# A graph layer's edge sort: scan operands moved to PSUM in three pieces, sums in a bank of their own, nodes to be normed in three buffers

## The chip, the cores and the metric

The kernel runs on one core of one Trainium2 chip. A time is the device time of one execution in microseconds. TensorE is PE in the profile (PEld is its loading of weights), VectorE is DVE, ScalarE is ACT, GpSimd is POOL and SyncE is SP. Each engine works through its own queue in order and waits on semaphores; SP only issues DMAs here, ACT and POOL issue some too.

## The reference

One layer of a graph network over N = 12,500 nodes of 64 features and E = 212,500 edges:

```python
h = jnp.maximum(_layernorm(x, axis=-1), 0.0)
edge_in = jnp.concatenate([h[row], h[col], dist], axis=1)      # row = src, col = dst
e = jax.nn.silu(edge_in @ eW1 + eb1)
e = jax.nn.silu(e @ eW2 + eb2)
agg = jax.ops.segment_sum(e, row, num_segments=h.shape[0])
out = jax.nn.silu(jnp.concatenate([h, agg], axis=1) @ nW1 + nb1) @ nW2 + nb2
return x + out
```

The edges come sorted by `dst`, while the sums go by `src`; `dist` is `edge_weight1`. The hidden width is 128.

## The kernel before, in words

**Node tables.** The nodes stand in NB = 100 buckets of L = 125 (node n is in bucket n mod 100). For twelve buckets at a time `normed` loads rows of x into one of two buffers `xs`, and norms them (`norm`: mean L531, difference L534, squares on ScalarE L535, variance, L543). `products` then turns four buckets (transposes L550, copy L554) and multiplies them with the two halves of eW1 (L180). The half for `src` is written out as three BF16 parts (`ta`, L598), that for `dst` as F32 (`tb`, L591). These generators, nine groups of twelve buckets, form the `feed`; `groups` lists them and `turns` takes a step of up to three of them in turn. The load of the next group stands in the same generator as its norm: it is issued, and the norm's first instruction is recorded one step later.

**Sending edges to their bucket.** The edges are cut into 208 blocks of 1024, and the blocks into 11 chunks (8 blocks, then 20 each). For a block, `count` compares (L308 makes `pick`, L309 makes `oh`, one row for each of the 100 buckets with a one where an edge belongs to that bucket), runs a scan along the block (L319, `run`: how many edges of this chunk the bucket has had so far, in two halves of 512), and multiplies the scan with `oh` (L323, `own`: the rank of each edge in its bucket's row). `send` sums `own` over the buckets with eight small matmuls (L342, into eight columns of `misc`), adds the bucket's base (L362, `to`: the row in DRAM to write), makes each edge's first-layer part from its `dst` node's row and its weight (L350, L357, L366), and scatters 128 edges an instruction to `q` in DRAM with GpSimd's indirect DMA (L371, 1,661 in all). `to` has four buffers, `qs` eight.

**The sums.** When all scatters of a chunk have landed, its 25 batches of four buckets are fetched (L416 the edges, L421 the `src` table) and go through a pipeline of steps of four tiles: `s_lr` and `s_one_t` (L439, L444) build the one-hot of `src`, `s_pt` (L453, L460) adds the parts of the first layer, ScalarE applies SiLU (L464), `s_p2` is the second layer (L492, L496), `s_one` (L473) a one-hot of the other orientation, `s_seg` (L504) sums the messages by node into PSUM, and `s_add` (L515) adds a batch's sums to `aggT` in SBUF. With the last chunk the node network runs too (`nodes`). Chunk c is summed while chunk c + 1 and later ones are counted and sent.

**Order.** PE, DVE, ACT and SP run in the order in which the program records them. The main loop walks over a list `turn` of pipeline steps with four hooks (`None`); at a hook it records pieces of `count` and `send` as far as a line between `marks` says, and two steps of the `feed`. A piece pairs one step of `count(s + 1)` with one of `send(s)`: in the first L308 and L309 with the rank matmuls, in the second the first half's scan and product with L350, L362 and four scatters, in the third the other half with four scatters. Ahead of the loop, chunk 0 and nine pieces of chunk 1 are recorded with four steps of the `feed` each.

**PSUM.** All eight banks are in use: `mm` four, `p2` two, and two of the pool `sgp`. In one of these stands the tile `misc`, which holds the sums of `s_seg` (500 columns, named `seg`) and the ranks (8 columns); in the other `run` (512 columns). Waits are made for tiles, so that one part of `misc` waits for the other. `nil`, a column of zeros and the scan's second input, is in SBUF.

Of the kernel before, what the change touches and what calls it, by code (L numbers as in the profile page):

```python
# [28 lines left out]
F32 = mybir.dt.float32  # L29
# [4 lines left out]
OP = mybir.AluOpType  # L34
# [4 lines left out]
P = 128  # L39
L = 125  # L40
WL = 48
HB = 64
BLK = 1024
HALF = BLK // 2
TB = BLK // P
PAIR = 2 * BLK
G = 4
# [12 lines left out]
def tile_gnn(ctx: ExitStack, tc: tile.TileContext, x, src, dst, ew, eW1, eb1, eW2, eb2, nW1, nb1, nW2, nb2, out):  # L60
    nc = tc.nc
    N, D = x.shape
    H = eW2.shape[0]
    E = src.shape[0]
    assert D == 64 and H == P and N % L == 0
    NB = N // L
# [40 lines left out]
    CH = 12  # L107
# [19 lines left out]
    for a in range(2):  # L127
        half = slice(a * D, (a + 1) * D)
# [62 lines left out]
    for win in wins:  # L191
        nc.vector.memset(win, 0.0)
        for a in range(2):
            for i, row in enumerate((w1d, eb1b)):
                at = a * HB + WL + i
# [40 lines left out]
    cnt = ctx.enter_context(tc.tile_pool(name="cnt", bufs=1))  # L236
    qsp = ctx.enter_context(tc.tile_pool(name="qs", bufs=8))
    top = ctx.enter_context(tc.tile_pool(name="to", bufs=4))
    with ExitStack() as work:
        mm = work.enter_context(tc.tile_pool(name="mm", bufs=4, space=PSUM))  # L240
        p2p = work.enter_context(tc.tile_pool(name="p2", bufs=2, space=PSUM))
        sgp = work.enter_context(tc.tile_pool(name="sg", bufs=1, space=PSUM))
# [2 lines left out]
                engines={mybir.EngineType.PE, mybir.EngineType.DVE, mybir.EngineType.Activation, mybir.EngineType.SP}  # L245
            )
        )
        misc = sgp.tile([P, G * L + TB], F32, name="misc")
        seg = misc[:, : G * L].rearrange("p (b l) -> p b l", l=L)
        rank = misc[:, G * L :]  # L250
        run = sgp.tile([NB, HALF], F32, name="run")
        oh = cnt.tile([NB, BLK], F16, name="oh")
        nil = cnt.tile([NB, 1], F32, name="nil")
        nc.vector.memset(nil, 0.0)
        carry = {}
        blk = {}
        nblocks = -(-E // BLK)
# [44 lines left out]
        def count(s):  # L302

            if s >= nblocks:
                return
            c = chunk_of[s]
            bc, bb, win, pick = blk[s]
            nc.vector.tensor_scalar(pick, bc, same, plus, op0=OP.is_equal, op1=OP.add)  # L308
            nc.vector.tensor_scalar(oh, bb[:NB, :], part[:NB, :], None, op0=OP.is_equal)  # L309
            yield  # L310
            weights(s)
            own = wk.tile([NB, BLK], F16, name="own")
            blk[s].append(own)
            for h in range(2):
                half = slice(h * HALF, (h + 1) * HALF)
                n = min(HALF, E - s * BLK - h * HALF)
                if n <= 0:
                    break
                nc.vector.tensor_tensor_scan(  # L319
                    run, oh[:, half], nil.to_broadcast([NB, HALF]), carry.get(c, -1.0), op0=OP.add, op1=OP.add  # L320
                )
                end = carry[c] = run[:, n - 1 : n]
                nc.vector.tensor_tensor(own[:, half], run, oh[:, half], op=OP.mult)  # L323
                if h == 0:
                    yield
            if s + 1 == nblocks or chunk_of[s + 1] != c:
                u = wk.tile([NB, 1], F32, name="u")
                for limit, op in ((chunks[c][2] * P - 1, OP.is_gt), (chunks[c][3] - 1, OP.is_lt)):
                    nc.vector.tensor_scalar(u, end, float(limit), None, op0=op)
                    nc.vector.tensor_tensor(bad[:NB, 1:2], bad[:NB, 1:2], u, op=OP.add)  # L330
            yield
# [70 lines left out]
        batch, st = {}, {}  # L402
# [3 lines left out]
        def fetch(i):  # L406
            if i >= len(batches):
                return
            c, B, n = batches[i]
            assert pending[c] == 0  # L410
            while B not in done_a:
                next(feed)
            q = chunks[c][-1]
            at = B * G * n * P
            qt = ld2.tile([P, G * most, W], F32, name="qt")
            nc.sync.dma_start(  # L416
                qt[:, : G * n, :].rearrange("p j w -> p (j w)"),
                q[at : at + G * n * P, :].rearrange("(p j) w -> p (j w)", p=P),
            )
            a3 = ld2.tile([P, G, 3, H], BF16, name="a3")  # L420
            nc.sync.dma_start(  # L421
                a3.rearrange("l b s f -> l b (s f)"), ta_buckets[:, B * G : B * G + G]
            )
            batch[c, B] = [qt, a3]
            if c == len(chunks) - 1:
                node_in[B] = nodes_in(B, ndp[0])

        def of(k):

            c, B, n, g = steps[k]  # L430
            return batch[c, B], [((g * G + t) % n * G + (g * G + t) // n, (g * G + t) // n) for t in range(G)]

        def s_lr(k):
            (qt, _), tiles = of(k)
            loc = qt.rearrange("p j w -> p (j w)").bitcast(BF16)
            lr = mm.tile([P, G, P], F32, name="lr", tag="mm")
            for t, (j, _) in enumerate(tiles):
                at = 2 * (j * W + H) + 1
                nc.tensor.matmul(lr[:L, t, :], loc[:, at : at + 1].to_broadcast([P, L]), identb, start=True, stop=True)  # L439
            st[k] = {"lr": lr}  # L440
# [5 lines left out]

        def s_pt(k):

            (qt, a3), tiles = of(k)
            oneT = st[k].pop("oneT")  # L450
            pt = mm.tile([P, G, P], F32, name="pt", tag="mm")
            for t, (j, _) in enumerate(tiles):
                nc.tensor.matmul(  # L453
                    pt[:, t, :], qt[:, j, :H], ident, is_transpose=True, start=t == 0, stop=False, skip_group_check=True
                )
            for b, same in itertools.groupby(range(G), lambda t: tiles[t][1]):
                same = list(same)
                cols = slice(same[0], same[-1] + 1)
                for i in range(3):
                    nc.tensor.matmul(  # L460
                        pt[:, cols, :], a3[:L, b, i, :], oneT[:, cols, :], start=False, stop=i == 2, skip_group_check=True
                    )
            e1 = wk.tile([P, G, P], F32, name="e1")
            nc.scalar.activation(e1, pt, AF.Silu)  # L464
            st[k]["e1"] = e1

        def s_one(k):
            (qt, _), tiles = of(k)
            c, B, n, g = steps[k]
            wide = [P, G // n, n, L]  # L470
            loc = qt[:, : G * n, H : H + 1].rearrange("p (j b) w -> p b j w", b=G)
            one = wk.tile([P, G, L], F32, name="one")
            nc.vector.tensor_tensor(  # L473
                one.rearrange("p (b j) l -> p b j l", j=n),
                nodes1[:, None, None, :].to_broadcast(wide),
                loc[:, tiles[0][1] : tiles[0][1] + G // n].to_broadcast(wide),
                op=OP.is_equal,
            )
            st[k]["one"] = one
            if g == n - 1:  # L480
                fetch(c * (NB // G) + B + NQ)
# [16 lines left out]

        def s_seg(k):
            c, B, n, g = steps[k]  # L500
            _, tiles = of(k)
            e2, one = st[k].pop("e2"), st[k].pop("one")
            for t, (j, b) in enumerate(tiles):
                nc.tensor.matmul(seg[:, b, :], e2[:, t, :], one[:, t, :], start=j < G, stop=j >= G * (n - 1))  # L504

        def s_add(k):
            c, B, n, g = steps[k]
            if g < n - 1:
                return
            v = aggT[:, B * G : B * G + G, :]  # L510
            del batch[c, B]
            if c == 0:
                nc.vector.tensor_copy(v, seg)
            else:
                nc.vector.tensor_tensor(v, v, seg, op=OP.add)  # L515
            if c == len(chunks) - 1:
                tails.append(nodes(B, *node_in.pop(B), mm, ndp[1], "mm"))
# [46 lines left out]
            nc.sync.dma_start(tb0.rearrange("(p j) f -> p j f", j=NE)[:, g : g + G, :], got)  # L564
            yield

        def normed(b0, n, xs):
            for part_ in (slice(0, 112), slice(112, L)):
                nc.sync.dma_start(xs[part_, :n, :], x_rows[part_, b0 : b0 + n, :])
            yield  # L570
            yield from norm(xs, n)
            yield
            ready.add(b0)
# [111 lines left out]
        def groups():  # L685

            starts = list(range(0, NB, CH))
            size = lambda b0: min(CH, NB - b0)
            todo = [normed(0, size(0), xss[0])]
            for i, b0 in enumerate(starts):  # L690
                todo += [(b0, products(b0, g, xss[i % 2])) for g in range(0, size(b0), G)]
                if i + 1 < len(starts):
                    at = len(todo) - size(b0) // G + 1
                    todo.insert(at, normed(starts[i + 1], size(starts[i + 1]), xss[(i + 1) % 2]))
            return todo

        done_a, done_b, ready = [], [], set()
        feeding = ExitStack()
        fp = feeding.enter_context(tc.tile_pool(name="fp", bufs=3, side="right"))
        fp1 = feeding.enter_context(tc.tile_pool(name="fp1", bufs=1, side="right"))  # L700
        xss = [fp1.tile([P, CH, D], F32, name=f"xs{i}") for i in range(2)]
        for xs in xss:
            nc.gpsimd.memset(xs, 0.0)

# [2 lines left out]
        with tc.tile_pool(name="lists", bufs=1, side="right") as lp:  # L707
# [4 lines left out]
            f, sf, t = (lp.tile([NP, PAIR], F32, name=n) for n in ("f", "sf", "t"))  # L712
# [54 lines left out]
        for c in range(1, len(chunks)):  # L767
            start = c * (NB // G) - NQ
# [178 lines left out]
```

## Time and profile before

| | us |
|---|---|
| median of three runs (lowest to highest) | 2692.52 (2691.67 to 2700.41) |
| the profiled execution | 2686.15 |
| its span, first to last instruction | 2684.3 |
| PE / PEld / DVE / ACT / POOL busy | 2246.3 / 2083.4 / 1959.1 / 1249.9 / 1831.5 |
| first and last scatter (L371) begin | 63.3 and 2435.8 |
| granted TensorE clock, mean | 0.917 |

In a line of a group, the busy time and the mean of one instruction (ns) come first after the bar, then the idle time of that engine just ahead of them and what ended most of it. In a line of waits the numbers are the total, how often, and the longest. A line of the timeline gives start, duration, instruction, and in brackets the idle time before it. A busy share is a mean over stages, and a wait is put down to whichever awaited event came last.

### The profile page before, as it was taken

The page shows a single profiled execution, that of the slowest core. Times are in us where ns is not written, and L with a number is a line of the kernel's source. Part 1 is how long each engine was busy: PE and PEld are TensorE (multiplying, and loading weights), DVE is VectorE, ACT ScalarE, POOL GpSimd, SP SyncE. Part 2 cuts the span into 40 slices and gives each one's busy share as a digit, 9 for nine tenths or more (in the row PEclk, how much of TensorE's full clock was granted, in tenths as well). Part 3 has the DMA queues.
Part 4 walks back from the last instruction along what each step waited for, and adds up shares of the span by engine and source line. Part 5 has one row for each costly group of instructions (what it writes and reads, how often), then busy time and mean ns, then how long its engine had stood idle before and what let it go on. Part 6 is the DMA issues. An engine that isn't in the chain of part 4 may idle for free.

```text
span 2684.3 us, 59579 instructions
## 1 busy us (share of the span) xinstructions
PE 2246.3 (84%) x21814; PEld 2083.4 (78%) x21814; DVE 1959.1 (73%) x3050; ACT 1249.9 (47%) x2687; POOL 1831.5 (68%) x1728
## 2 busy tenths in 40 slices
PE   2444786888998998799799889989889989997997
PEld 2333676887887888798788888879878889897896
DVE  5765896877887878698688778878768878773443
ACT  2333643544554545354355445445435545553443
POOL 3564777777777777777777777777777777773000
PEclk9855887988998999899899999989989999998999
DMA  8776779658767866976876786696687666664441
GB/s 204 194 211 214 228 233 278 213 194 235 237 211 224 264 198 210 261 230 209 236 234 217 229 260 203 204 279 214 206 245 232 218 208 220 208 205 165 152 165 53
DMA packets 257973, 577.22 MB, mean 215 GB/s; under 512 B 51201, under 2 KB 110579, under 8 KB 257468
## 3 DMA queue, kind: packets, MB, share of 16 engines
q1 hardware_dynamic: 185096, 384.91, 44.6%
q0 software_dynamic: 54144, 123.04, 13.0%
q10 hardware_dynamic: 18434, 65.37, 10.6%
q8 instruction: 176, 2.88, 0.5%
q14 instruction: 123, 1.01, 0.1%
HBM read 361.44 MB, written 211.67 MB: 214 GB/s over the span
## 4 chain that ended last, share of the span: by engine, by line
PE 38%; DMA 28%; POOL 15%; issue 8%; DVE 6%; ACT 3%; SPq 2%; ACTq 0%; DVEq 0%; POOLq 0%
DMA q<-qs,to 18%; POOL q L371 15%; PE misc L504 9%; PE p L492 8%; PE pt L460 6%; PE pt L453 4%; DMA pick<-in_edge_weight_dram 4%; PE qp L350 4%; PE lr L439 2%; DMA xs<-in_x_dram 2%; DMA a<-ta 1%; DVE run L319 1%; DVE oneT L444 1%; ACT qs L357 1%; PE ab L180 1%
## 5 line engine op out<-in xcount | busy, mean ns | idle before, releaser
L371 POOL DMA_INDIRECT q<-qs,to x1661 | 1793.4, 1080 | 603.3 <-issue 415.4
L504 PE MATMUL misc<-one,e 128*128 128x125 f32 x4200 | 595.9, 287 | 155.5 <-DVE to L362 127.1
L464 ACT ACTIVATE e<-pt 128x512 f32<-128x512 f32 x525 | 313.7, 597 | 823.5 <-PE pt L460 764.1
L504 PEld LDWEIGHTS misc<-one,e 128*128 128x128 f32 x4200 | 535.9, 200 | 171.0 <-issue 130.3
L492 PE MATMUL p<-w,e 128*128 128x128 f32 x4200 | 592.0, 286 | 0.0
L492 PEld LDWEIGHTS p<-w,e 128*128 128x128 f32 x4200 | 535.2, 200 | 24.6 <-issue 9.7
L319 DVE TENSOR_TENSOR_SCAN run<-oh,run,nil 100x512 f32<-100x512 f16 x405 | 523.1, 1292 | 0.2
L444 DVE TENSOR_SCALAR oneT<-lr,part 125x512 bf16<-125x512 f32 x525 | 391.5, 746 | 140.3 <-PE lr L439 135.8
L460 PE MATMUL pt<-oneT,a 125*128 125x256 bf16 (+1 forms) x3300 | 454.7, 278 | 0.0
L357 ACT COPY qs<-qp 128x512 f32<-128x512 f32 x416 | 230.5, 587 | 389.8 <-PE qp L350 212.7
L453 PE MATMUL pt<-ident,qt 128*128 128x128 f32 x2100 | 341.0, 287 | 30.6 <-DVE oneT L444 29.1
L460 PEld LDWEIGHTS <-a 125*128 125x128 bf16 x3300 | 325.6, 102 | 38.9
L473 DVE TENSOR_TENSOR one<-nodes,qt 128x500 f32<-128x500 f32 x525 | 352.5, 671 | 0.5 <-PE misc L504 0.5
L350 PE MATMUL qp<-win,pick 50*128 50x128 f32 x3322 | 263.9, 299 | 69.6 <-DMA pick<-in_edge_weight_dram 41.9
L496 ACT ACTIVATE e<-p 128x512 f32<-128x512 f32 x525 | 313.9, 598 | 16.4 <-PE p L492 15.8
L486 ACT COPY p<-b2f 128x512 f32<-128x512 f32 x525 | 312.0, 594 | 0.1
L350 PEld LDWEIGHTS qp<-win,pick 50*128 50x128 f32 x3322 | 223.0, 201 | 101.5 <-issue 82.2
L323 DVE TENSOR_TENSOR own<-run,oh 100x512 f16<-100x512 f32 x416 | 287.7, 691 | 14.2
L515 DVE TENSOR_TENSOR aggT<-aggT,misc 128x500 f32<-128x500 f32 x250 | 167.6, 670 | 149.7 <-PE misc L504 111.2
L453 PEld LDWEIGHTS pt<-ident,qt 128*128 128x128 f32 x2100 | 234.8, 148 | 36.4 <-DVE oneT L444 32.3
L439 PE MATMUL lr<-identb,qt 128*125 128x128 bf16 x2100 | 219.4, 229 | 19.2 <-DMA qt<-q 19.2
L439 PEld LDWEIGHTS <-qt 128*125 128x125 bf16 x2100 | 193.1, 143 | 30.3 <-DMA qt<-q 19.6
(122 smaller groups left out, 1095.6 us busy)
## 6 DMA issues: line engine op xcount, KB each, us to landing
qt<-q SPq DMA_DIRECT2D x250, 576.0 KB
a<-ta SPq DMA_DIRECT2D x275, 384.0 KB
q<-zeros ACTq DMA_DIRECT2D x30, 1638.0 KB
bb<-rows SPq DMA_DIRECT2D x208, 224.0 KB
bc<-rows SPq DMA_DIRECT2D x208, 128.0 KB
q<-qs,to POOLq DMA_INDIRECT x1661
win<-tb SPq DMA_DIRECT2D x416, 24.0 KB
ta<-parts SPq DMA_DIRECT2D x25, 384.0 KB
```

The source lines that it names most:

```text
L319: nc.vector.tensor_tensor_scan(run, oh[:, half], nil.to_broadcast([NB, HALF]), carry.get(c, -1.0), op0=OP.add, op1=OP.add)
L350: nc.tensor.matmul(qps[a][:, t, :], pick[half, t * P : (t + 1) * P], win[half, :], start=True, stop=True)
L371: i = nc.gpsimd.indirect_dma_start(out=q[:], out_offset=bass.IndirectOffsetOnAxis(ap=to[:k, t : t + 1], axis=0), in_=qs[:k, t - t0, :], in ...
L439: nc.tensor.matmul(lr[:L, t, :], loc[:, at : at + 1].to_broadcast([P, L]), identb, start=True, stop=True)
L444: nc.vector.tensor_scalar(oneT, st[k].pop("lr")[:L], part1[:L, :], None, op0=OP.is_equal)
L453: nc.tensor.matmul(pt[:, t, :], qt[:, j, :H], ident, is_transpose=True, start=t == 0, stop=False, skip_group_check=True)
L460: nc.tensor.matmul(pt[:, cols, :], a3[:L, b, i, :], oneT[:, cols, :], start=False, stop=i == 2, skip_group_check=True)
L464: nc.scalar.activation(e1, pt, AF.Silu)
L473: nc.vector.tensor_tensor(one.rearrange("p (b j) l -> p b j l", j=n), nodes1[:, None, None, :].to_broadcast(wide), loc[:, tiles[0][1] : ti ...
L492: nc.tensor.matmul(p2[:, t, :], e1[:, t, :], w2, start=False, stop=t == G - 1, skip_group_check=True)
L496: nc.scalar.activation(e2, p2, AF.Silu)
L504: nc.tensor.matmul(seg[:, b, :], e2[:, t, :], one[:, t, :], start=j < G, stop=j >= G * (n - 1))
```

## The change

`seg` becomes a tile of its own in the pool `sgp`, made for each batch at its first step. `run` takes its place in `misc`: that tile now holds `run`, 342 columns wide (a third of a block), the eight ranks, and `nil`, which a memset at the start fills. The scan and the product of a block run in three pieces of 342, 342 and 340 columns, the first in the piece where the first half was, the other two in the next. The last, short block is scanned over its whole tiles only.

The load of a group is a generator of its own, `loaded`; there are three buffers `xs`. The first two groups are loaded at the start, and group i + 2 ahead of the products of group i. A batch's record gets a third field for `seg`, for which three unpackings are changed.

```diff
-        misc = sgp.tile([P, G * L + TB], F32, name="misc")
-        seg = misc[:, : G * L].rearrange("p (b l) -> p b l", l=L)
-        rank = misc[:, G * L :]
-        run = sgp.tile([NB, HALF], F32, name="run")
+        CUT = -(-BLK // 3)
+        misc = sgp.tile([P, CUT + TB + 1], F32, name="misc")
+        run, rank, nil = misc[:NB, :CUT], misc[:, CUT : CUT + TB], misc[:NB, CUT + TB :]
+        nc.vector.memset(nil, 0.0)
         oh = cnt.tile([NB, BLK], F16, name="oh")
-        nil = cnt.tile([NB, 1], F32, name="nil")
-        nc.vector.memset(nil, 0.0)
...
-            for h in range(2):
-                half = slice(h * HALF, (h + 1) * HALF)
-                n = min(HALF, E - s * BLK - h * HALF)
-                if n <= 0:
-                    break
+            n = min(BLK, E - s * BLK)
+            full = -(-n // P) * P
+            for at in range(0, full, CUT):
+                m = min(CUT, full - at)
+                cols = slice(at, at + m)
                 nc.vector.tensor_tensor_scan(
-                    run, oh[:, half], nil.to_broadcast([NB, HALF]), carry.get(c, -1.0), op0=OP.add, op1=OP.add
+                    run[:, :m], oh[:, cols], nil.to_broadcast([NB, m]), carry.get(c, -1.0), op0=OP.add, op1=OP.add
                 )
-                end = carry[c] = run[:, n - 1 : n]
-                nc.vector.tensor_tensor(own[:, half], run, oh[:, half], op=OP.mult)
-                if h == 0:
+                last = min(m, n - at)
+                end = carry[c] = run[:, last - 1 : last]
+                nc.vector.tensor_tensor(own[:, cols], run[:, :m], oh[:, cols], op=OP.mult)
+                if at == 0:
                     yield
...
-            _, tiles = of(k)
+            item, tiles = of(k)
+            if g == 0:
+                item[2] = sgp.tile([P, G, L], F32, name="seg")
             e2, one = st[k].pop("e2"), st[k].pop("one")
             for t, (j, b) in enumerate(tiles):
-                nc.tensor.matmul(seg[:, b, :], e2[:, t, :], one[:, t, :], start=j < G, stop=j >= G * (n - 1))
+                nc.tensor.matmul(item[2][:, b, :], e2[:, t, :], one[:, t, :], start=j < G, stop=j >= G * (n - 1))
...
-        def normed(b0, n, xs):
+        def loaded(b0, n, xs):
             for part_ in (slice(0, 112), slice(112, L)):
                 nc.sync.dma_start(xs[part_, :n, :], x_rows[part_, b0 : b0 + n, :])
             yield
+
+        def normed(b0, n, xs):
             yield from norm(xs, n)
...
-            todo = [normed(0, size(0), xss[0])]
+            of = [(b0, size(b0), xss[i % len(xss)]) for i, b0 in enumerate(starts)]
+            todo = [loaded(*of[0]), loaded(*of[1]), normed(*of[0])]
             for i, b0 in enumerate(starts):
-                todo += [(b0, products(b0, g, xss[i % 2])) for g in range(0, size(b0), G)]
+                if i + 2 < len(starts):
+                    todo.append((b0, loaded(*of[i + 2])))
+                todo += [(b0, products(b0, g, of[i][2])) for g in range(0, size(b0), G)]
                 if i + 1 < len(starts):
-                    at = len(todo) - size(b0) // G + 1
-                    todo.insert(at, normed(starts[i + 1], size(starts[i + 1]), xss[(i + 1) % 2]))
+                    todo.insert(len(todo) - size(b0) // G + 1, normed(*of[i + 1]))
...
-        xss = [fp1.tile([P, CH, D], F32, name=f"xs{i}") for i in range(2)]
+        xss = [fp1.tile([P, CH, D], F32, name=f"xs{i}") for i in range(3)]
```

More of the change, by code (lines that the diff above doesn't have):

```diff
@@ L423, in fetch @@
             )
-            batch[c, B] = [qt, a3]
+            batch[c, B] = [qt, a3, None]
             if c == len(chunks) - 1:
@@ L433, in s_lr @@
         def s_lr(k):
-            (qt, _), tiles = of(k)
+            (qt, _, _), tiles = of(k)
             loc = qt.rearrange("p j w -> p (j w)").bitcast(BF16)
@@ L447, in s_pt @@
         def s_pt(k):
-            (qt, a3), tiles = of(k)
+            (qt, a3, _), tiles = of(k)
             oneT = st[k].pop("oneT")
@@ L467, in s_one @@
         def s_one(k):
-            (qt, _), tiles = of(k)
+            (qt, _, _), tiles = of(k)
             c, B, n, g = steps[k]
@@ L510, in s_add @@
             v = aggT[:, B * G : B * G + G, :]
-            del batch[c, B]
+            seg = batch.pop((c, B))[2]
             if c == 0:
```

## The prediction

> **What bounds the kernel now.** I read the engine table and slices first: PE 84%, VectorE (DVE) 73%, GpSimd (POOL) 68% with the same 7 in every slice from the fifth to the thirty-seventh. An engine that is even for 2,000 us is a candidate even at 68%. So next come its group and, from the view by source line, the spread of its durations:
>
> ```profile
> L371 POOL DMA_INDIRECT q<-qs,to x1661 | 1793.4, 1080 | 603.3 <-issue 415.4
> ...
> L319 DVE TENSOR_TENSOR_SCAN run<-oh,run,nil 100x512 f32<-100x512 f16 x405 | 523.1, 1292 | 0.2
> ...
> L323 DVE TENSOR_TENSOR own<-run,oh 100x512 f16<-100x512 f32 x416 | 287.7, 691 | 14.2
> ```
> ```profile
> L371 POOL DMA_INDIRECT q<-qs,to x1661: 887/967/2049, 63.3 to 2435.8; - x185
> ```
> One scatter of 128 edges takes 967 ns at the median, 1080 in the mean, and about 0.30 us of "issue" stands ahead of nearly every one. Then the waits, in total over the run:
>
> ```profile
> DVE to L362 <- DMA q<-qs,to: 198.1, 81, 9.4
> ...
> PE misc L504 <- DVE to L362: 127.1, 51, 9.6
> ...
> DVE aggT L515 <- PE misc L504: 111.2, 74, 5.2
> ...
> DVE mean L531 <- DMA xs<-in_x_dram: 56.7, 9, 15.4
> ...
> DVE aggT L515 <- PE misc L342: 36.8, 34, 4.0
> ```
> VectorE waits for scatters (`to` has four buffers), and TensorE's sums (L504) wait for that VectorE instruction: backpressure from POOL. The sends of chunks 2 to 10 run from 439 to 2437 us, 222 us for 160 scatters, and POOL's gaps there beyond the constant 0.305 us add up to 16 us in 1,998. So POOL is the bound there. The windows by engine show how much room the others have (columns: PE, PEld, DVE, ACT, POOL busy, clock, DMA share, GB/s):
>
> ```profile
> 300.00:440.00 140.00, 104.33 (x1038) 95.89 (x1036) 109.83 (x173) 66.64 (x155) 108.36 (x98) 0.81 0.78 242
> ...
> 1109.00:1331.00 222.00, 196.18 (x1980) 184.26 (x1980) 174.86 (x270) 107.59 (x230) 171.01 (x159) 0.95 0.73 228
> ...
> 2226.00:2405.00 179.00, 171.61 (x1766) 162.63 (x1764) 148.47 (x229) 95.77 (x202) 139.77 (x129) 0.99 0.65 214
> 2405.00:2684.00 279.00, 249.37 (x2159) 226.37 (x2157) 106.26 (x175) 115.39 (x229) 42.94 (x50) 0.96 0.42 136
> ```
> Last, why 1080 and not 967. The timeline at 1402 us:
>
> ```profile
> 1402.11 0.96 POOL L371 DMA_INDIRECT q<-qs,to  x1 [0.30 <-issue]
> ...
> 1405.47 1.29 DVE L319 TENSOR_TENSOR_SCAN run<-oh,run,nil 100x512 f32<-100x512 f16 x1
> 1406.00 1.52 POOL L371 DMA_INDIRECT q<-qs,to  x1 [0.30 <-issue]
> 1406.79 0.69 DVE L323 TENSOR_TENSOR own<-run,oh 100x512 f16<-100x512 f32 x1
> ```
> The scatter that begins inside a scan takes 1.52 us. Sorting all 1,661 by what VectorE ran when they began: 401 began in a scan and lie 308 ns above 967 on average (123.5 us); 187 began in `one` (L473, two SBUF inputs) at 195 ns (36.5 us); the rest hold 28 us. Those that begin in the sum L515, with one input in PSUM, lie about 30 ns above. So it is an instruction with two SBUF inputs that delays a scatter.
>
> **The change part by part.** Sums are made against this execution's span, 2684.3 us.
>
> *Scan reads `nil` from PSUM.* It then has one SBUF input, as L323 and L515 have. Taken: the 123.5 us go. By busy time of L371 less 967 ns a scatter, chunks 2 to 10 hold 154 of the 188 us of excess, so 123.5 × 154/188 = 101 us there, 11 a chunk: POOL's pace goes from 222 to 211 us. The other 22 lie in chunks 0 and 1. Bounds: 0 (the delay stays), and 148 in all, which is what comes out if scatters are sorted by what runs 0.5 us after their start. [...]
>
> *Three pieces for two.* [...] The scan's read of PSUM is not in this trace. [...]
>
> *Sums in their own bank.* L504 no longer waits for `to`, nor L515 for the rank matmuls L342. The first is POOL's backpressure, no gain by itself, but 127 us (11 a chunk) of PE idle that need not lie there: PE is busy 198 a chunk at clock 0.95, and other waits on VectorE and the weights (28 us at L453, 22 at L350, 14 at L504 from 440 to 2436) make 7, so 205 in 211. It fits, barely; 171.61 of 179 us in the window before 2405 shows that PE can run at 96%. The second frees 36.8 us of VectorE.
>
> *`run` and ranks now share a bank.* In the built program 111 of 208 first scans of a block carry a wait for TensorE (its rank matmuls of the block before); until now `to`, which stands right behind, had it (12 us of idle over the run). Behind it on VectorE stand the product, `to`, then oneT, for which TensorE waits. [...]
>
> These margins are thin, so I do not give the whole of 11: I estimate 2 us a chunk lost to engines waiting for each other. **Chunks 2 to 10: 9 × 9 = −81 us.**
>
> *Loads a group ahead.* Each mean L531 stands behind its own load: 52.8 us over 8 loads from 117 to 324 us, with the scan and `to` of the next block queued behind. POOL shows it: gaps over 1 us between 126 and 301 us add up to 48. A load has some 30 us now. Its two DMAs still stand on SP's queue in front of `pick` and `tb`, and wait for TensorE's transposes of an older group, so not later than now; the memset of the third buffer (0.76 us) falls into POOL's idle time before 63 us. Other steps of the same chain (L554, L590) are behind part of the gaps. I take 30 of the 48, and 10 of the 22 us of scan delay, as POOL isn't the bound throughout: **−40**, between 0 and −70.
>
> The tail after the last scatter (247 us: last chunk's edges and the nodes, with PE busy 249 of 279) has no scans: 0. Sum: −121, span 2563. The median of the runs shown is 8.2 us above this span (2692.52; the profiled execution itself took 2686.15), so **2571**.
>
> **Rivals.**
> *PE becomes the bound* with chunks at 217: 9 × 5 + 40 = 85, 2608. For it: 198 busy of 211. Against: it holds 96% before 2405.
> [...]
> *Slower: the shared bank.* Each block's first scan waits until TensorE, in its own order, comes to the rank matmuls. [...] For it: L515's 1.08 us. Against: `to` had this wait and idled 12 us.
>
> **How the numbers follow.** Forecast 0.56, own range 2530 to 2600 (no friction and 60 from the loads, or double friction and 25); PE 0.20; delay stays 0.13, of which 0.04 with no change; shared bank or a slow PSUM scan 0.09; 0.02 I can't name, shared out. A measurement of this kernel tells about 0.3% from no change. Faster 0.87, same 0.04, slower 0.09. The range reaches from the bound of the scan's delay with all of the loads (−120 − 60, 2515) to the delay that stays (2660).
>
> **What would show it.** L371's mean below 1010 ns, its median still 967, no long scatter inside a scan. The scan 937 ns, the product 514. Sends of a chunk in 210 to 215 us. No L504 wait for `to`; L531 without its load. Wrong: L371's mean still over 1060; the scan above 1.2 us; a wait of the scan for L342 above 1 us a block.

## The result, and the profile after

The changed kernel takes 2590.12 us in the median of four runs (2588.91 to 2591.15), the kernel before 2692.1 beside it (2685.22 to 2700.41): a ratio of 0.962, 95% interval 0.9592 to 0.9647. That is 102 us less, where 121 were forecast. The span of the profiled execution went from 2684.3 to 2588.4 us, 96 less. (On another chip, where TensorE is granted 0.82 of its clock for 0.93 here and stands still for 523 us, the same change lengthens the kernel by 2.6%; that is in the experiments.)

The groups of the changed kernel that answer to those shown of before (after the bar: busy time, mean in ns, idle time ahead and its cause):

```profile
L370 POOL DMA_INDIRECT q<-qs,to x1661 | 1697.4, 1022 | 602.7 <-issue 397.5
...
L317 DVE TENSOR_TENSOR_SCAN misc<-oh,misc 100x342 f32<-100x342 f16 (+1 forms) x623 | 579.7, 930 | 9.3 <-PE misc L341 1.2
...
L322 DVE TENSOR_TENSOR own<-misc,oh 100x342 f16<-100x342 f32 (+1 forms) x623 | 320.0, 514 | 21.6
```
```profile
L370 POOL DMA_INDIRECT q<-qs,to x1661: 887/967/1839, 63.7 to 2339.2; - x185
```
A scatter costs 967 ns at the median as before, and 1022 in the mean for 1080. The last begins at 2339 us for 2436: all of the gain lies ahead of it. Scan and product take 930 and 514 ns a third. The waits (total, times, longest):

```profile
DVE to L361 <- DMA q<-qs,to: 149.3, 81, 7.3
...
DVE aggT L516 <- PE seg L505: 93.9, 66, 4.2
...
PE seg L505 <- DVE aggT L516: 42.5, 65, 1.7
...
DVE mean L532 <- DMA xs<-in_x_dram: 2.8, 1, 2.8
...
DVE misc L317 <- PE misc L341: 1.2, 1, 1.2
```
The sums no longer wait for `to`, and the wait of the first norms for their load has gone from 56.7 to 2.8 us. The wait that had become possible, of the scan for the rank matmuls in its bank, happened once, for 1.2 us. That VectorE still waits 149 us for scatters says that POOL still leads. The timeline at 1101 us shows what a scan does to a scatter now:

```profile
1100.97 0.93 DVE L317 TENSOR_TENSOR_SCAN misc<-oh,misc 100x342 f32<-100x342 f16 x1
1101.50 0.97 POOL L370 DMA_INDIRECT q<-qs,to  x1 [0.30 <-issue]
...
1102.49 0.93 DVE L317 TENSOR_TENSOR_SCAN misc<-oh,misc 100x340 f32<-100x340 f16 x1
1102.77 0.96 POOL L370 DMA_INDIRECT q<-qs,to  x1 [0.30 <-issue]
...
1105.13 0.67 DVE L472 TENSOR_TENSOR one<-nodes,qt 128x500 f32<-128x500 f32 x1
1105.31 1.33 POOL L370 DMA_INDIRECT q<-qs,to  x1 [0.30 <-ACT p L485]
```
Two scatters begin inside a scan and take 0.97 us; the one that begins inside `one`, whose two inputs are still in SBUF, takes 1.33. Over the run 339 scatters begin in a scan, and their sum differs from 339 times 967 ns by 0.2 us (by 123.5 us before); 224 begin in `one`, and hold 58.4 us above 967 ns each (36.5 before, with 187).

The windows by engine (PE, PEld, DVE, ACT, POOL busy, clock, DMA share, GB/s) for a chunk in the middle, the last chunk's sends, and the tail:

```profile
1050.00:1266.00 216.00, 194.95 (x1970) 181.78 (x1971) 183.35 (x311) 106.89 (x229) 160.80 (x160) 0.97 0.75 236
2130.00:2340.00 210.00, 195.41 (x2019) 186.50 (x2019) 167.35 (x283) 110.39 (x232) 162.44 (x157) 0.98 0.61 201
2340.00:2588.00 248.00, 228.09 (x1951) 205.89 (x1951) 95.34 (x157) 103.18 (x204) 19.03 (x26) 0.96 0.43 140
```
Stage by stage, taken from the end of each chunk's last scatter:

| stage | before, us | after, us | difference | forecast |
|---|---|---|---|---|
| start to chunk 1 sent | 438.7 | 400.3 | −38.4 | −40 |
| chunks 2 to 10 | 1997.9 | 1939.8 | −58.1 | −81 |
| after the last scatter | 247.7 | 248.3 | +0.6 | 0 |
| span | 2684.3 | 2588.4 | −95.9 | −121 |

### The profile page after: what moved, and what is told of

It is laid out like the page before. It is cut to its first block, busy times and chain, and to the rows that moved or that the text cites. A ratio compares the mean times of both kernels' runs of the same rounds, so it can differ in the third digit from the quotient of the medians.

```text
span 2588.4 us, 60017 instructions
## 1 busy us (share of the span) xinstructions
PE 2205.0 (85%) x21814; PEld 2041.8 (79%) x21814; DVE 2034.8 (79%) x3464; ACT 1246.9 (48%) x2687; POOL 1736.8 (67%) x1729
## 4 chain that ended last, share of the span: by engine, by line
PE 40%; DMA 23%; DVE 13%; POOL 7%; issue 6%; ACT 2%; SPq 1%; DVEq 0%; ACTq 0%; POOLq 0%
DMA q<-qs,to 14%; PE seg L505 10%; PE p L491 9%; POOL q L370 7%; PE pt L459 7%; PE pt L452 5%; DVE misc L317 5%; PE qp L349 4%; PE lr L438 3%; DMA bc<-rows 2%; DVE oneT L443 2%; DMA bb<-rows 2%; DVE one L472 2%; DMA pick<-in_edge_weight_dram 2%; DVE own L322 2%
## 5 line engine op out<-in xcount | busy, mean ns | idle before, releaser
L370 POOL DMA_INDIRECT q<-qs,to x1661 | 1697.4, 1022 | 602.7 <-issue 397.5
L505 PE MATMUL seg<-one,e 128*128 128x125 f32 x4200 | 581.4, 282 | 54.7 <-DVE aggT L516 42.5
L317 DVE TENSOR_TENSOR_SCAN misc<-oh,misc 100x342 f32<-100x342 f16 (+1 forms) x623 | 579.7, 930 | 9.3 <-PE misc L341 1.2
L505 PEld LDWEIGHTS seg<-one,e 128*128 128x128 f32 x4200 | 524.4, 196 | 68.5 <-ACT p L485 27.7
L491 PEld LDWEIGHTS p<-w,e 128*128 128x128 f32 x4200 | 527.9, 197 | 31.0 <-issue 8.4
L443 DVE TENSOR_SCALAR oneT<-lr,part 125x512 bf16<-125x512 f32 x525 | 390.8, 744 | 111.1 <-PE lr L438 109.0
L459 PE MATMUL pt<-oneT,a 125*128 125x256 bf16 (+1 forms) x3300 | 443.0, 273 | 0.1
L452 PE MATMUL pt<-ident,qt 128*128 128x128 f32 x2100 | 332.0, 282 | 73.4 <-DVE oneT L443 73.4
L459 PEld LDWEIGHTS <-a 125*128 125x128 bf16 x3300 | 318.7, 100 | 35.5 <-issue 1.0
L322 DVE TENSOR_TENSOR own<-misc,oh 100x342 f16<-100x342 f32 (+1 forms) x623 | 320.0, 514 | 21.6
L516 DVE TENSOR_TENSOR aggT<-aggT,seg 128x500 f32<-128x500 f32 x250 | 166.9, 667 | 94.2 <-PE seg L505 93.9
```

Source lines behind the costliest of these rows:

```text
L317: nc.vector.tensor_tensor_scan(run[:, :m], oh[:, cols], nil.to_broadcast([NB, m]), carry.get(c, -1.0), op0=OP.add, op1=OP.add)
L322: nc.vector.tensor_tensor(own[:, cols], run[:, :m], oh[:, cols], op=OP.mult)
L370: i = nc.gpsimd.indirect_dma_start(out=q[:], out_offset=bass.IndirectOffsetOnAxis(ap=to[:k, t : t + 1], axis=0), in_=qs[:k, t - t0, :], in ...
L443: nc.vector.tensor_scalar(oneT, st[k].pop("lr")[:L], part1[:L, :], None, op0=OP.is_equal)
L452: nc.tensor.matmul(pt[:, t, :], qt[:, j, :H], ident, is_transpose=True, start=t == 0, stop=False, skip_group_check=True)
L459: nc.tensor.matmul(pt[:, cols, :], a3[:L, b, i, :], oneT[:, cols, :], start=False, stop=i == 2, skip_group_check=True)
```

## The experiments

The theory to be tested has two parts: a VectorE instruction with two SBUF inputs delays the scatters that begin during it, which set the pace; and the early loads are a gain of their own. The rivals: the loads give most of the gain; the scan delayed scatters by its length or by its write to PSUM; the bank of its own for the sums is what counts; VectorE's additional work has eaten much of the gain.

**The scan's part alone, and the loads alone.** The first is the changed kernel with `loaded` and `groups` put back and two buffers, the second the kernel before with that part of the diff. (Only the line of the buffers is shown here.)

```diff
-        xss = [fp1.tile([P, CH, D], F32, name=f"xs{i}") for i in range(3)]
+        xss = [fp1.tile([P, CH, D], F32, name=f"xs{i}") for i in range(2)]
```


> The changed kernel with the loads of the kernel before (two buffers, load and norm in one generator). Theory (scan no longer delays scatters; loads are a gain of their own): the mean of the scatter L370 near 1022 ns as in the changed kernel, sends of chunks 3 to 9 in 215 to 217 us, but chunks 0 and 1 sent later, first to last scatter up to chunk 1 about 360 us for 337; in all 2612 to 2628 us. Rival (most of the gain is from the loads, the scan gave what the three pieces cost): 2650 us or more.

> The kernel before with only the loads changed (three buffers, a group ahead). Theory: L371 still 1080 ns in the mean, 222 us a chunk from chunk 2 on, chunks 0 and 1 sent some 25 us earlier; 2662 to 2672 us. Rival (the scatters' queue catches up by itself, the loads are hidden): 2689 to 2695 us.

Measured beside 2691.14 us for the kernel before: 2631.11 us for the scan's part (ratio 0.9776, 0.975 to 0.9802), 2663.6 us for the loads (0.9893, 0.987 to 0.9915). The scan's part, from its group and waits:

```profile
L370 POOL DMA_INDIRECT q<-qs,to x1661 | 1702.3, 1025 | 640.7 <-issue 400.5
```
```profile
DVE mean L532 <- DMA xs<-in_x_dram: 55.2, 9, 15.0
```
and the loads:

```profile
L371 POOL DMA_INDIRECT q<-qs,to x1661 | 1805.9, 1087 | 568.8 <-issue 402.6
```
```profile
DVE mean L531 <- DMA xs<-in_x_dram: 3.2, 1, 3.2
```
Each part does its own work: the one frees the scatters and leaves the wait for the load, the other the reverse. In chunks 2 to 10 the scan's part takes 1941.8 us, as the changed kernel (1939.8), the loads 2002.6. Up to the end of chunk 1 it is the other way round: 441.3 us for the scan's part (438.7 before), 411.6 for the loads, 400.3 with both. So at the start freed scatters are worth nothing while VectorE waits for x (POOL's gaps in chunk 1 grow from 38.5 to 55.4 us), and 11 us when it doesn't. That is why the parts give 60 and 27.5 us alone and 102 together. The rival that the loads give most of the gain falls, and so does the one that they are hidden anyway. The time of the scan's part lies 3 us above the range expected for it.

**Only nil back in SBUF.** The changed kernel, with this alone:

```diff
-        misc = sgp.tile([P, CUT + TB + 1], F32, name="misc")
-        run, rank, nil = misc[:NB, :CUT], misc[:, CUT : CUT + TB], misc[:NB, CUT + TB :]
+        misc = sgp.tile([P, CUT + TB], F32, name="misc")
+        run, rank = misc[:NB, :CUT], misc[:, CUT : CUT + TB]
+        nil = cnt.tile([NB, 1], F32, name="nil")
```


> The changed kernel, in which only nil goes back to SBUF (three pieces, sums in their own bank and the loads stay). Theory (it is the second SBUF input that delays a scatter): 401 x 2814/2584 = 437 scatters begin in a scan, each delayed by 308 x 937/1292 = 223 ns, 97 us in all; the mean of the scatter near 1080 ns, 220 to 224 us a chunk, 2655 to 2675 us. Rival (the delay came from the scan's length of 1.29 us or from its write to PSUM beside the sums): as the changed kernel, 1022 ns and 2585 to 2595 us.

Measured: 2666.83 us (0.9916, 0.9892 to 0.994), within the theory's range, as is the mean of the scatter. (Of the sum behind it the product came out, 90 us for 97, and not its factors: 276 scatters begin in a scan and are held for 324 ns each, where 437 and 223 were expected.) Its groups:

```profile
L371 POOL DMA_INDIRECT q<-qs,to x1661 | 1797.7, 1082 | 575.9 <-issue 406.3
...
L318 DVE TENSOR_TENSOR_SCAN misc<-oh,misc,nil 100x342 f32<-100x342 f16 (+1 forms) x612 | 573.1, 936 | 9.2 <-PE misc L342 1.2
```
and its timeline:

```profile
1113.95 0.93 DVE L318 TENSOR_TENSOR_SCAN misc<-oh,misc,nil 100x342 f32<-100x342 f16 x1
1114.14 1.50 POOL L371 DMA_INDIRECT q<-qs,to  x1 [0.30 <-issue]
```
The scan is as short as in the changed kernel, and writes to the same place in PSUM; one column of zeros in SBUF brings back the mean of 1082 ns and 2005.7 us for chunks 2 to 10. So the scan's second SBUF input is the cause, and neither its length nor its write. With three pieces and a bank for the sums, but with the delay, chunks 2 to 10 are no faster than before (1997.9): these two parts gain nothing by themselves where POOL leads. Nor does it lengthen the scan that its zeros come from PSUM: 930 ns against 936 from SBUF.

**The node numbers in PSUM as well.** The changed kernel, with the other frequent instruction of two SBUF inputs, `one`, relieved in the same manner:

```diff
-        misc = sgp.tile([P, CUT + TB + 1], F32, name="misc")
+        misc = sgp.tile([P, CUT + TB + 1 + L], F32, name="misc")
+        nodes_p = misc[:, CUT + TB + 1 :]
+        nc.vector.tensor_copy(nodes_p, nodes1)
...
-                nodes1[:, None, None, :].to_broadcast(wide),
+                nodes_p[:, None, None, :].to_broadcast(wide),
```


> The changed kernel, in which the node numbers that one (L472) compares with also lie in PSUM, beside run, ranks and nil: one then has one SBUF input, too. Theory (any VectorE instruction with two SBUF inputs delays scatters): of the 92.6 us that scatters take above 967 ns, the 58 that begin in one go, the mean falls from 1022 to about 985 ns; POOL's pace for a chunk goes to 209 us and the time to 2555 to 2580 us, unless the new waits of one for the rank matmuls, and of these for one, take it back (2590 to 2620 us, at a mean of 985 all the same). [...]

Measured: 2559.04 us (0.9517, 0.9494 to 0.9541), the fastest of all, 31 us below the changed kernel. Its scatters, and what the shared bank costs now:

```profile
L372 POOL DMA_INDIRECT q<-qs,to x1661 | 1637.0, 986 | 624.2 <-issue 406.0
```
```profile
PE misc L343 <- DVE one L474: 88.9, 90, 4.0
```
The mean falls to 986 ns, as forecast to 1 ns, and what begins in `one` holds 4.9 us for 58.4. So the mechanism isn't one of scans. Of the 55 us that scatters in chunks 2 to 10 save (74.2 to 19.1 above the median), 33 reach the end of the sends (1939.8 to 1907.2); the rest goes into POOL's gaps, which grow from 39 to 62 us. Rank matmuls now wait 89 us for `one`, which reads their bank.

Nor are two SBUF inputs the only form that delays. Of the 31 us that all scatters of this run still take above 967 ns, those that begin in `oh` hold 8.4 (50 scatters, 168 ns each) and those that begin in `pick` 7.3, which often has `oh` behind it; `oh` compares a single SBUF tensor with a column of numbers:

```profile
663.96 0.47 DVE L309 TENSOR_SCALAR oh<-bb,part 100x1024 f16<-100x1024 bf16 x1
664.12 1.15 POOL L372 DMA_INDIRECT q<-qs,to  x1 [0.30 <-issue]
```
What in `oh` delays them was not tested.

**Three changes that want TensorE's or VectorE's time, and other chips.** The first puts the zeros with sums and ranks in one bank (the kernel before, with `misc` one column wider and `nil` in it). The second is the changed kernel with four pieces (`CUT = -(-BLK // 4)`). The third is the last experiment's kernel, node numbers in PSUM included, with the ranks in a buffer of the pool `mm` of four banks:

```diff
+            rank = mm.tile([P, TB], F32, name="rank", tag="mm")
             for t in range(nt):
                 nc.tensor.matmul(rank[:, t : t + 1], run[:, t * P : (t + 1) * P], fours[:NB, :], start=True, stop=True)
```


> The kernel before (two halves of 512, sums and ranks in one bank, its loads), in which only nil moves to PSUM, into the bank of sums and ranks. To be held against the scan part alone (e1_scan, 2631 us), which has the bank for the sums and three pieces in addition. Theory: the scatters are freed all the same (mean about 1025 ns), but each scan now waits for the sums' matmuls and these for the scan; at about 1 us for each of 40 scans a chunk VectorE goes to 175 + 19 + 40 = 234 us a chunk, and the time to 2690 to 2800 us. Rival (the bank of its own for the sums gives nothing, VectorE does with two pieces better than with three): 2610 to 2631 us.

> The changed kernel with four pieces of 256 for three of 342: one more pair of scan and product, 387 ns a block, 7.7 us of VectorE a chunk, 80 us in all. Theory (VectorE has 202 of 215 us and room for it): 2590 to 2605 us, chunks within 1 us of the changed kernel's 215.5. Rival (VectorE is on the path already, and the three pieces took back what the freed scatters would have given): 2640 to 2670 us.

> The kernel with run, nil and the node numbers in one bank (e5_nodes_psum), in which the ranks move to a buffer of the pool mm, so that TensorE writes nothing into that bank. Theory: the 89 us that rank matmuls waited for one go, the gaps of POOL beyond its constant 0.305 us from 54 to 20 to 40 us in chunks 2 to 10, the scatter's mean stays near 985 ns; 2535 to 2555 us. Rival (the ring of four banks is short of one for part of the time, and TensorE waits for ScalarE and VectorE to empty them): 2560 to 2600 us.

They ran on a chip on which the kernel before takes 3479.82 us. Measured: 3670.56 us (1.0543, 1.0465 to 1.0621), 3554.32 us (1.0215, 1.0142 to 1.0287) and 3730.28 us (1.0711, 1.0637 to 1.0786). The times expected were for a chip like the first one, so the same three kernels ran again:

> The kernel of e4_nil_with_sums once more, on a chip on which the kernel before takes near 2692 us. Theory: the scatters are freed (mean about 1025 ns), but each scan waits for the sums' matmuls and these for the scan, and the time goes to 2690 to 2800 us. Rival (the bank of its own for the sums gives nothing): 2610 to 2631 us.

> The kernel of e6_four_pieces once more, on a chip on which the kernel before takes near 2692 us. Theory (VectorE has room for 7.7 us more a chunk): 2590 to 2605 us. Rival (VectorE is on the path already): 2640 to 2670 us.

> The kernel of e8_rank_mm once more, on a chip on which the kernel before takes near 2692 us. Theory: the 89 us that rank matmuls waited for one go, POOL's gaps in chunks 2 to 10 fall from 54 to 20 to 40 us; 2535 to 2555 us. Rival (the ring of four banks is short of one): 2560 to 2600 us, and where it is TensorE that waits, more than that.

That was yet another chip, with 3492.48 us for the kernel before: 3673.03 us (1.0521), 3568.71 us (1.0237) and 3728.45 us (1.0682). The last two runs ask what such a chip does with the change itself:

> The changed kernel beside the next one. Where the kernel before takes near 2692 us on the chip: 2590 us again. Where it takes near 3485 us, since TensorE stands still at its own issue for some 550 us and sets the pace, theory: freed scatters are worth nothing there (POOL waits for the others 900 us anyway), and what the change costs VectorE and TensorE remains; 3440 to 3520 us, with 20 to 40 us of the loads at most as a gain. Rival (the gain is not tied to POOL's pace): 3380 us or less.

> The changed kernel with four pieces of 256 for three of 342, beside the changed kernel itself. Theory where POOL sets the pace (2692 us before): within 10 us of the changed kernel, since VectorE has room for 7.7 us more a chunk; rival: 50 to 80 us above it. Theory where TensorE sets the pace (3485 us before): the same, within 20 us of the changed kernel, at 3550 to 3570 us, which then itself would lie near 3550; rival: the changed kernel near 3485, the fourth piece 80 us.

It was a third chip of this kind, with 3486.94 us for the kernel before. The changed kernel takes 3571.07 us (1.0259, 1.0209 to 1.031), where 3440 to 3520 were expected; with four pieces it takes 3555.62 us (1.0208, 1.016 to 1.0257). The changed kernel there, in a window as long as a chunk, and its waits:

```profile
1400.00:1716.00 316.00, 258.21 (x1988) 227.55 (x1989) 184.04 (x309) 109.66 (x231) 164.41 (x162) 0.82 0.51 164
```
```profile
POOL q L370 <- ACT qs L365: 872.3, 149, 23.6
...
PE qp L349 <- issue: 152.1, 231, 3.6
...
PE p L491 <- issue: 114.6, 189, 1.7
```
A chunk takes 316 us for 216 with the same work. VectorE's and POOL's busy times are the same (184 and 164 us), TensorE's is 258 for 195, and its clock 0.82 for 0.97: over the run it is granted half speed for 1,306 us, against 387 in the run shown above, and stands still for 523 us ahead of matmuls that wait for nothing the profile shows (`issue`; 10 us there). In the window shown these standstills come to 48 us, which with the 258 busy ones make 306 of 316: TensorE sets the pace. POOL waits 872 us for the rows to scatter. On such a chip the theory's gain must vanish, and it does; but the change is 2.6% slower, which nothing here had forecast. VectorE's additional work doesn't explain it: the third piece costs 366 ns a block (three times 930 and 514 ns for twice 1292 and 691), a fourth 0.35 us more (four times 0.75 and 0.42 us), and with it the kernel is 15 us faster, not 80 slower. The 387 ns a block and VectorE's 202 us a chunk in the expectations were the author's estimates, which no run shows; the 366 ns, and 196 us in the changed kernel where POOL leads, stand in their place. The granted clock doesn't settle it either: 0.819 to 0.835 in the runs of the kernel before, 0.809 to 0.817 with the change, but 0.811 to 0.835 with four pieces, which are slower than before all the same. A profile of the kernel before on such a chip is not among these runs, so the cause stays open.

The three kernels answer their questions only in part on such chips. With the zeros beside the sums the scatters are freed: 213 begin in a scan that is as long as the old one, and their sum differs from 213 times 967 ns by 0.1 us. But the scan pays. The lines are from the second run; the lower one is of the scans without a start value:

```profile
L319 DVE TENSOR_TENSOR_SCAN run<-oh,run,misc 100x512 f32<-100x512 f16 x405 | 521.6, 1288 | 283.6 <-PE misc L504 208.0
...
L319 DVE TENSOR_TENSOR_SCAN run<-oh,misc 100x512 f32<-100x512 f16 x11 | 13.5, 1225 | 7.0 <-PE misc L504 7.0
```
VectorE idles 284 us ahead of its scans (60 in the changed kernel on such a chip), 208 of it for the sums. So the sums' own bank is what makes room for the zeros in PSUM: no gain by itself, but without it the scan would be tied to TensorE. What that costs where POOL leads wasn't measured. That a fourth piece costs nothing is shown for these chips alone. Whether ranks in `mm` pay isn't shown at all: that kernel is the slowest, at 3728 to 3730 us, but it has the node numbers in PSUM too, and the kernel with these alone didn't run on such a chip.

## Why the prediction was right

*What bounds the kernel.* Right: POOL's scatters set the pace from chunk 2 on, which the loads-alone and nil-in-SBUF runs show from both sides (1080 to 1087 ns and some 2,000 us; 1022 to 1025 ns and some 1,940).

*Scan reads nil from PSUM, −101 us in chunks 2 to 10.* The mechanism was right, the term too large: scatters there hold 74.2 us above their median for 155.3, so 81 went. Those that began in a scan held 105 us there, and all of it went. The step that failed is a silent one, that the other delays stay as they are: in these chunks `one` took back 23 us (57 for 34). Over the run more scatters began in it than before (224 for 187), each held for 261 ns (195). Two readings of the trace before were off besides. Scatters that begin in the sum L515 lie at 967 ns and not 30 above, which helps the argument; and the "rest" of 28 us that was passed over holds 10.8 us of scatters that begin in `oh` (64, at 168 ns), so that the conclusion on two SBUF inputs was too narrow. The nil-in-SBUF and node-number runs bear the mechanism out: 1082 ns with the zeros back in SBUF, 986 with the node numbers in PSUM as well.

*Three pieces.* Right: 930 and 514 ns for 937 and 514. The 937 and 514 were the author's estimate, from a rate and fixed times that the trace of before doesn't show. What the runs show is a scan with a start value of 1292 ns at 512 columns, 930 at 342 and 0.75 us at 256, with a product of 691 ns, 514 ns and 0.42 us. In the window of a chunk VectorE is busy for 183 us, after 175 in one of before, and from 401 to 2340 us it waits 70.6 us at L443 and 49.7 at L516 for TensorE, 13 a chunk: 196 of 216, so three pieces fit. To read zeros from PSUM costs the scan nothing, as taken: without a start value 512 columns take 1225 ns with them in PSUM (nil beside the sums) as in SBUF. The trace of before had the like of it in two other instructions of 500 columns, 670 ns for the sum L515 with one input in PSUM and 671 for `one` (L473) with both in SBUF.

*Friction, 2 us a chunk.* POOL's gaps in chunks 2 to 10 rose from 16 to 39 us, 23 for the 18 taken. The 2 us were an allowance for thin margins that no row gave, so that they came near is partly luck. With −81 for the scatters the 23 give −58, the measured difference.

*Shared bank.* The scan waited once for the rank matmuls, 1.2 us; the row of L515 (1.08 us a wait) misled, since TensorE had passed the rank matmuls 2.5 us, in the median, before the next block's first scan came.

*Loads, −40.* −38.4, and split as taken: 27 by the loads alone and 11 more from freed scatters (30 and 10 in the forecast).

*Rivals.* TensorE as the bound at 217 us a chunk was nearer than its 0.20 says: chunks came in at 215.5, but VectorE still waited 138 us for scatters in that stretch, so POOL kept the lead. On the other chips TensorE does set the pace, and there the change even loses, which the forecast had only for the shared bank or a slow scan.

## What to carry to other kernels

When a queue of scatters on GpSimd sets the pace, look at the spread of its durations, not at the mean, and sort the long ones by what VectorE was doing: here a column of zeros moved to PSUM, and node numbers after it, took 1080 ns to 986. Freeing one delay can move part of it to the next of its kind (from the scan to `one` here), so count every instruction that delays before sizing the gain: here the scan and `one`, with two SBUF inputs (308 and 195 ns a scatter before), and `oh`, with one tensor (168). A gain that comes from one engine's lead holds only where that engine leads: where TensorE set the pace here, at a clock of 0.82, the same edit lost 2.6%.

## What was not expected of the hardware

The chips differed: the kernel before took 2685 to 2700 us beside the result and the first four experiments, and 3462 to 3510 on three other chips. On one of these the changed kernel ran at a mean TensorE clock of 0.82 for 0.93, and TensorE stood still for 523 us without a wait. No chip was measured twice, so whether this lies in the chip or in its state at the time isn't shown.

VectorE can be the one that is held, too. `oh` takes 0.48 us in the median, but in the changed kernel 86 of 208 take some 0.7, all of them among those that begin 0.5 us or more after a scatter's start, while it still runs; none of the 18 that begin while no scatter runs does:

```profile
1105.31 1.33 POOL L370 DMA_INDIRECT q<-qs,to  x1 [0.30 <-ACT p L485]
...
1106.17 0.69 DVE L307 TENSOR_SCALAR oh<-bb,part 100x1024 f16<-100x1024 bf16 x1
```
